# One graph-attention kernel on one core: transposes grouped ahead of their copies, layer 1's value loads on ScalarE's queue, pools in another order, late tiles started two steps apart

## The chip, the cores and the metric

The kernel runs on one core of one Trainium2 chip. The metric is the device time of one launch in microseconds (us). A profile is one further execution taken by the hardware profiler; its times count from the start of its span. The engines are TensorE (PE, with its weight loads as PEld), VectorE (DVE), ScalarE (ACT), GpSimd (POOL) and SyncE (SP, which here only issues transfers). "SPq", "ACTq" and "POOLq" are the transfers that these engines issue.

## The reference

x is 2708 x 256, adj is 2708 x 2708 and sparse with a full diagonal. Two layers follow each other, each as `x = layernorm(x + layer(x, adj))`.

```python
# layer 0, two steps n of: top-p attention and a walk over the graph
q = Xa @ W1.T @ W2.T;  k = Xa @ W3.T
probs = softmax(q @ k.T)
A = probs cut to the smallest set of each row with mass 0.9, rows rescaled
R = adj + I, rows rescaled
Xf = R @ Xf;  Xa = A @ Xa
Z = Z + Xf @ U1[n].T + Xa @ U2[n].T
# after both steps: layernorm(x + Z) * g + b
# layer 1, four heads of 64: graph attention
Wh = einsum('nd,hdo->nho', x, W)
e = leaky_relu(s_i[:, None] + s_j[None, :])       # s_i, s_j: Wh times a
attention = softmax(where(adj != 0, e, -inf))
h_prime = einsum('ijh,jho->iho', attention, Wh)
```

## The kernel before

**Tiles.** The 2708 rows are cut into 22 tiles: 16 of 128 rows and 6 of 110. For transposes they are taken in groups of up to four tiles of the same height (`groups`, six of them). All matrix work is in float32; one matmul of the program shows as two records on PE.

**Layer 0, start.** `query_weights` (L606 on) folds W1 and W2. Then `turn_x` transposes x, group by group: for each of the two halves c of the 256 columns, up to four PE transposes write half c of a two-bank PSUM tile `lg`, and a copy brings that half to SBUF (c = 0 by ScalarE, c = 1 by VectorE, both L1091). `project` (L619 on) multiplies the turned group by the weights (L631) and copies keys out by VectorE (L635) and queries by ScalarE (L636). The loop turns group n + 1 before it projects group n, so that the PE has transposes while the copies of group n run. `lg` and the projections' PSUM tile `tr` have two buffers each.

**Layer 0, the two steps.** In each step, for each tile, PE turns the scores (L240) and multiplies (L258, `att`), with the walk's matmuls (L901) dealt out between; ScalarE, VectorE and GpSimd find the cut of the coming tiles. This runs from about 74 us to 1229 us.

**Late tiles.** Tiles 18 to 21 (`LATE = 4`) are not finished inside layer 0. Each is a generator, `prepared(t)` (L1330 on), and each call of `beside` (L1344 on) moves it one step. Six steps are two layer norms, done by ScalarE and GpSimd alone (`layernorm_beside`, L141 on, and `norms`, L181 on); the seventh transposes the tile's x on PE (L160) and copies it (L162); the eighth multiplies it by layer 1's weights (L166), after which ScalarE writes `sb`, `tj`, `s_src` and the four heads' values (L170 to L176) and stores the values to DRAM (L179). `verdict` (L1127 on) is a fifth generator, a check of layer 0's shortcuts, nearly all on VectorE. Before the change late tile k lets k calls pass and then starts, and `verdict` lets 4 pass.

**Layer 1.** Destinations are taken in three groups g of 8, 8 and 6 tiles; for each g all 22 source tiles j are gone through, two at a time ("a pair" below). `mask` (L1286 on) loads tile j's values `v[j]` from DRAM (only for g = 0, L1290) and then calls `neighbours`, which loads the block of adj (L1220) into one of three buffers `blk` and makes it 0 or 1 by two passes of ScalarE (Sign L1221, Square L1222). `weights` makes four tiles `pt` per source tile on VectorE (L1302), in a ring of three. `values` multiplies them by v (L1313), `denominators` by `sb` (L1323). A pair is: `beside`, `weights(n+2)`, `mask(n+3)`, values and denominators of both tiles, `beside`, `weights(n+3)`, `mask(n+4)`. So `beside` is called twice a pair, once at each side of the pair's matmuls.

**Who sets the order.** The lines run under a manual schedule for PE, ACT, DVE and POOL: within one such block each of these engines keeps the order of the program text. SP is not among them; where its transfers stand is the framework's choice, and so is how the two blocks (layer 0 and layer 1) are merged at their seam. In the program before, the first three blocks of adj are loaded and turned into masks while layer 0's last tile is still attended to.

**Pools.** SBUF pools lie one behind the other in the order in which they are opened. Layer 1's pools are opened after those of layer 0 are closed and lie over the same addresses; the first use of a new pool waits for the last uses of all old pools that it overlaps. Before: `pj` (the `pt` tiles) lies over part of w0, over keep (xm, qT, kT1) and over the front of tpp (the turned scores `eT`); `keep1` (the values v) lies over keepb (`ba`, the values of step 1's attention) and wk.

Of the kernel before, what the change touches and what calls it, by code (L numbers as in the profile page):

```python
# [37 lines left out]
HELD, WAITING = 6, 4  # L38
# [6 lines left out]
def kernel(  # L45
# [16 lines left out]
    nc = tc.nc  # L62
# [5 lines left out]
    NT = (N + P - 1) // P  # L68
# [48 lines left out]
    LATE = 4  # L117
# [37 lines left out]
    def sources(t, pool, room, queue=nc.sync):  # L155

        m = rows[t]
        tp = room()
        for c in range(DC):
            nc.tensor.transpose(tp[:, c, :m], xe[:m, t, c * P : (c + 1) * P], ident[:m, :m])  # L160
        xT = pool.tile([P, DC, P], F32, name="xT")
        nc.scalar.copy(xT[:, :, :m], tp[:, 0:DC, :m])  # L162
        yield
        wp = room().rearrange("p a b -> p (a b)")
        for c in range(DC):
            nc.tensor.matmul(  # L166
                wp[:m, : D + 2 * H], xT[:, c, :m], wx[:, c, :],
                start=(c == 0), stop=(c == DC - 1),
            )
        nc.scalar.activation(sb[:m, t, :], wp[:m, D : D + H], AF.Exp)  # L170
        nc.scalar.activation(tj[:m, t, :], wp[:m, D : D + H], AF.Exp, scale=NEG_SLOPE - 1.0)
        nc.scalar.copy(s_src[:m, t, :], wp[:m, D + H : D + 2 * H])
        vt = pool.tile([P, D], F32, name="cs")
        for h in range(H):
            cols = slice(h * FO, (h + 1) * FO)
            nc.scalar.activation(  # L176
                vt[:m, cols], wp[:m, cols], AF.Copy, scale=sb[:m, t, h : h + 1]
            )
        queue.dma_start(vd[t][:m], vt[:m])  # L179

    def norms(t, xt, norm=layernorm, other=None):  # L181

        m = rows[t]
        hh = xe[:m, t, 0:D]
        h2 = hh if other is None else other()[:m]
        yield from norm(h2, hh, m)
        nc.gpsimd.tensor_mul(h2, h2, g_sb[:m])  # L187
        nc.gpsimd.tensor_add(h2, h2, xt[:m])  # L188
        yield
        yield from norm(hh, h2, m)  # L190
        yield
        if t < NT - LATE:
            yield
# [331 lines left out]
    def fast_layer0(ep, adjp):  # L525

        l0 = ExitStack()

        heldp, finp, rowp, w0, keep, tpp, sortp, keepb, wk = (
            l0.enter_context(tc.tile_pool(name=name, bufs=bufs))  # L530
            for name, bufs in (
                ("heldp", HELD), ("finp", 2), ("rowp", 2), ("w0", 1), ("keep", 1),
                ("tpp", 3), ("sortp", 1), ("keepb", 1), ("wk", 1),
            )
        )
        ps_lg, ps_wk, ps_at, ps_tr = (
# [543 lines left out]
        def turn_x(grp):  # L1080
            k = rows[grp[0]]
            w, c0 = k * len(grp), off[grp[0]]
            tp = ps_lg.tile([P, 2, CHUNK], F32, name="lg")
            for c in range(DC):
                for q, t in enumerate(grp):
                    nc.tensor.transpose(
                        tp[:, c, q * k : (q + 1) * k], xm[:k, t, c * P : (c + 1) * P],
                        ident[:k, :k],
                    )
                copy = nc.vector.tensor_copy if c else nc.scalar.copy  # L1090
                copy(x_turned[:, c, c0 : c0 + w], tp[:, c, :w])  # L1091
            return c0, w

        with tc.manual_schedule(engines=engines):
            query_weights()
            ahead = turn_x(groups[0])
            for n in range(len(groups)):
                c0, w = ahead
                if n + 1 < len(groups):
                    ahead = turn_x(groups[n + 1])  # L1100
                pj = ps_tr.tile([P, 4, P], F32, name="tr").rearrange("p a b -> p (a b)")
                project(
                    0, c0, w, pj, x_turned[:, :, c0 : c0 + w],
                    nc.scalar.copy, nc.vector.tensor_copy,
                )
# [87 lines left out]
    def layer1(ep, adjp, r=None, verdict=None):  # L1193
        l1 = ExitStack()

        pp, pj, rp, keep = (
            l1.enter_context(tc.tile_pool(name=name, bufs=bufs))
            for name, bufs in (("pp", 2), ("pj", 1), ("rp", 1), ("keep1", 1))
        )
        DEEP = 3  # L1200
        ps_u = l1.enter_context(tc.tile_pool(name="ps_u", bufs=2, space=PSUM))
# [12 lines left out]
        def neighbours(g, j):  # L1214

            k = rows[j]
            i0, i1 = off[spans[g][0]], off[spans[g][-1] + 1]
            bar = adjp.tile([P, NT - HT, P], F32, name="blk")
            bar = bar.rearrange("p t d -> p (t d)")[:k, : i1 - i0]
            nc.sync.dma_start(bar, adjT[off[j] : off[j + 1], i0:i1])  # L1220
            nc.scalar.activation(bar, bar, AF.Sign)  # L1221
            nc.scalar.activation(bar, bar, AF.Square)  # L1222
            if j in spans[g]:
                own = bar[:, off[j] - i0 : off[j + 1] - i0]
                nc.vector.tensor_tensor(own, own, ident[:k, :k], op=ALU.max)
            return bar
# [59 lines left out]
        def mask(n):  # L1286
            if n < len(order):
                g, _, j = order[n]
                if g == 0:
                    nc.sync.dma_start(  # L1290
                        v[j][: rows[j]].rearrange("p h o -> p (h o)"), vd[j][: rows[j]]
                    )
                masks[n] = neighbours(g, j)
# [36 lines left out]
        def prepared(t):  # L1330

            yield from norms(
                t, x_late[:, t - NT + LATE, :], layernorm_beside,
                lambda: pp.tile([P, D], F32, name="h2", bufs=4),
            )
            yield from sources(t, pp, aux, nc.scalar)


        late = []
        if verdict:  # L1340
            late += [[k, prepared(NT - LATE + k)] for k in range(LATE)]
            late.append([LATE, verdict(aux)])
        rest, running = [], []
        def beside(g, i):  # L1344

# [19 lines left out]
        for n in range(DEEP):  # L1365
            mask(n)
# [3 lines left out]
        for n in range(0, len(order), 2):  # L1370
            g, i, j = order[n]
            beside(g, i)
            weights(n + 2)
            mask(n + 3)
            if i == 0:
                acc = [
# [7 lines left out]
            for u in (n, n + 1):  # L1384
                for k in range(2):
                    values(u, (2 * k, 2 * k + 1))
                    if last and u > n:
                        for c, (c0, w) in enumerate(cuts[g]):
                            copy = nc.scalar.copy if c == 0 else nc.vector.tensor_copy
# [3 lines left out]
            if last:  # L1393
                for c, (c0, w) in enumerate(cuts[g]):
                    copy = nc.scalar.copy if c == 0 else nc.vector.tensor_copy
# [3 lines left out]
            else:  # L1399
                beside(g, i + 1)  # L1400
            weights(n + 3)
            mask(n + 4)
        assert not late

# [10 lines left out]
    with ExitStack() as both:  # L1415

        adjp = both.enter_context(tc.tile_pool(name="adjp", bufs=3))
        ep = both.enter_context(tc.tile_pool(name="ep", bufs=3))
        left = fast_layer0(ep, adjp)
        with tc.manual_schedule(engines=engines):  # L1420
            layer1(ep, adjp, *left)
    flag = nc.values_load(bad[0:1, 0:1])
    with tc.If(flag > 0):
        general_layer0()
        with ExitStack() as again:
            adjp = again.enter_context(tc.tile_pool(name="adjp", bufs=3))
            ep = again.enter_context(tc.tile_pool(name="ep", bufs=3))
            layer1(ep, adjp)
# [45 lines left out]
```

## Time and profile before

Three runs took 1595.8, 1595.95 and 1597.88 us; the median is 1595.95 us. The profiled execution took 1593.14 us, its span is 1591.3 us.

| engine | busy us | share of the span | instructions |
|---|---|---|---|
| PE | 1542.3 | 97% | 8029 |
| DVE | 1202.5 | 76% | 3651 |
| ACT | 798.9 | 50% | 1462 |
| POOL | 429.1 | 27% | 884 |

How to read it: PE is busy nearly all the time, so time is lost or won where it is not: at the start (before 34 us), at the seam between the layers (about 1229 to 1345 us) and at the very end. The rows of groups by line have the busy time, the mean of one, and the idle time before them with what ended it. In the timeline, equal instructions that follow each other are one row: start, length, engine, line, operation, tiles, how many records, and in brackets the idle time before the row and what ended it. A granted clock below 1.00 in a stretch means that PE ran slower for a part of it.

### The profile page before, as it was taken

The numbers are of one execution on the slowest core, as the hardware profiler recorded it, in microseconds if no ns is written. First come the engines' busy times: TensorE is split into PE (matmuls) and PEld (weight loads), VectorE is DVE, ScalarE is ACT, GpSimd is POOL, SyncE is SP. The second block draws the span as 40 slices with busy tenths as digits, with TensorE's granted clock in tenths as the row PEclk, the third lists the DMA queues.
The fourth block names the chain that finished last, engine by engine and source line by source line (L and its number), as shares of the span: only waits on it lengthen the run. The fifth ranks groups of instructions, "written<-read, shape, count | busy, mean of one in ns | idle before, by whom it ended". The sixth has DMA issues, their size and how long they took to land. (4 is left out here: it accounts for less than half of the span.)

```text
span 1591.3 us, 23822 instructions
## 1 busy us (share of the span) xinstructions
PE 1542.3 (97%) x8029; PEld 1037.7 (65%) x8029; DVE 1202.5 (76%) x3651; ACT 798.9 (50%) x1462; POOL 429.1 (27%) x884
## 2 busy tenths in 40 slices
PE   6999999999998999999999999999999999999994
PEld 3477777777776888787787788887787333333342
DVE  2777677767408876878779888888884978999995
ACT  2444444444335455555555556556643454456473
POOL 1311000000022222232224454534441720033133
PEclk9999999999999999999999999999999999999997
DMA  5200000000134333333333334433344434334331
GB/s 139 78 13 14 12 9 12 10 9 10 42 94 124 86 100 82 98 76 78 80 102 94 100 107 107 111 104 93 78 101 130 130 102 139 93 105 133 85 100 43
DMA packets 172494, 128.27 MB, mean 81 GB/s; under 512 B 44342, under 2 KB 161804, under 8 KB 172362
## 3 DMA queue, kind: packets, MB, share of 16 engines
q1 hardware_dynamic: 165030, 114.63, 26.9%
q0 software_dynamic: 3648, 9.26, 1.8%
q10 hardware_dynamic: 3684, 2.76, 0.5%
q8 instruction: 65, 1.06, 0.3%
q14 instruction: 67, 0.55, 0.1%
HBM read 111.78 MB, written 13.46 MB: 79 GB/s over the span
## 5 line engine op out<-in xcount | busy, mean ns | idle before, releaser
L245 ACT COPY eT<-tr 128x512 f32<-128x512 f32 (+5 forms) x264 | 141.2, 535 | 275.8 <-PE tr L240 273.1
L686 ACT ACTIVATE junk<-e,minus,rth 128x2708 bf16<-128x2708 f32 (+1 forms) x88 | 232.8, 2646 | 36.1 <-POOL rth L718 35.2
L258 PE MATMUL att<-xm,eT 128*128 128x256 f32 (+3 forms) x968 | 230.9, 380 | 0.4 <-ACT xa L1030 0.4
L258 PE MATMUL att<-ba,eT 128*128 128x256 f32 (+3 forms) x968 | 230.8, 379 | 0.3 <-ACT eT L245 0.2
L901 PE MATMUL walk<-xe,blk 128*128 128x257 f32 (+3 forms) x968 | 225.3, 384 | 5.0 <-DVE xf L915 5.0
L901 PE MATMUL walk<-xm,blk 128*128 128x256 f32 (+3 forms) x968 | 222.0, 380 | 1.0 <-DVE xw L974 1.0
L1313 PE MATMUL acc<-pt,v 128*64 128x512 f32 (+3 forms) x1056 | 216.3, 555 | 2.4 <-DMA v<-v 2.2
L901 PEld LDWEIGHTS walk<-xe,blk 128*128 128x128 f32 (+3 forms) x968 | 178.5, 187 | 50.3 <-issue 12.6
L1302 DVE SCALAR_TENSOR_TENSOR pt<-e,tj,blk 128x1024 f32<-128x1024 f32 (+3 forms) x176 | 187.1, 1128 | 20.3 <-PE att L258 8.7
L901 PEld LDWEIGHTS walk<-xm,blk 128*128 128x128 f32 (+3 forms) x968 | 177.7, 186 | 34.5 <-issue 4.9
L258 PEld LDWEIGHTS att<-xm,eT 128*128 128x128 f32 (+3 forms) x968 | 169.6, 186 | 22.1 <-ACT xa L1030 0.8
L258 PEld LDWEIGHTS att<-ba,eT 128*128 128x128 f32 (+3 forms) x968 | 169.5, 186 | 22.0 <-ACT eT L245 0.8
L665 ACT ACTIVATE e<-lg 128x1024 f32<-128x1024 f32 (+1 forms) x132 | 121.0, 921 | 110.6 <-PE lg L661 107.0
L1313 PEld LDWEIGHTS acc<-pt,v 128*64 128x64 f32 (+1 forms) x1056 | 75.6, 139 | 133.2 <-issue 107.5
L766 DVE MAX8 cand<-e 128x8 f32<-128x170 f32 (+1 forms) x352 | 89.6, 323 | 90.5 <-ACT e L665 90.4
L240 PEld LDWEIGHTS tr<-ident,e 128*128 128x128 f32 (+3 forms) x968 | 115.1, 138 | 56.3 <-issue 21.0
L240 PE MATMUL tr<-ident,e 128*128 128x128 f32 (+3 forms) x968 | 147.1, 271 | 0.7 <-ACT xe L952 0.3
L1302 DVE SCALAR_TENSOR_TENSOR pt<-r,tj,blk 128x1024 f32<-128x1024 f32 (+1 forms) x88 | 110.0, 1313 | 5.8 <-PE acc L1323 3.0
L1323 PE MATMUL acc<-pt,sb 128*32 128x512 f32 (+3 forms) x1056 | 106.8, 545 | 0.0
L766 DVE MAX8 cand<-scr 128x8 f32<-128x97 f32 (+1 forms) x616 | 102.3, 245 | 0.0
L1221 ACT ACTIVATE blk<-blk 128x1024 f32<-128x1024 f32 (+3 forms) x66 | 63.1, 956 | 70.2 <-DMA blk<-in_adjT_dram 57.1
L915 DVE TENSOR_TENSOR xf<-walk,xe 128x257 f32<-128x257 f32 (+1 forms) x22 | 9.4, 426 | 110.8 <-PE walk L901 110.8
(237 smaller groups left out, 1976.2 us busy)
## 6 DMA issues: line engine op xcount, KB each, us to landing
blk<-in_adjT_dram SPq DMA_DIRECT2D x32, 704.0 KB
blk<-in_adjT_dram SPq DMA_DIRECT2D x32, 512.0 KB
blk<-in_adjT_dram SPq DMA_DIRECT2D x48, 330.0 KB
blk<-in_adjT_dram SPq DMA_DIRECT2D x32, 320.0 KB
blk<-in_adjT_dram SPq DMA_DIRECT2D x12, 605.0 KB
blk<-in_adjT_dram SPq DMA_DIRECT2D x12, 440.0 KB
blk<-in_adjT_dram SPq DMA_DIRECT2D x18, 283.6 KB
c<-cs POOLq DMA_DIRECT2D x32, 128.0 KB, 2.0
```

Of the source, the lines that this page charges most:

```text
L240: nc.tensor.transpose(tr[: rows[t], q, :m], e[:m, off[t] : off[t + 1]], ident[:m, :m])
L245: copy(eT[:k, : len(grp), :m], tr[:k, : len(grp), :m])
L258: nc.tensor.matmul(acc, eT[: rows[t], q, :m], value(t), start=(t == 0), stop=(t == NT - 1),)
L665: nc.scalar.activation(halves[:m, :, c0 : c0 + w], lg[:m, :, :w], AF.Exp, accum_out=zp[:m, n : n + 1],)
L686: nc.scalar.activation(junk[:m], e[:m], func, scale=rth, bias=minus1[:m], accum_out=acc)
L766: nc.vector.max(cand[:, n, :], src[:m, n * size : min(N, (n + 1) * size)])
L901: nc.tensor.matmul(ac[:m, :w], blk[: rows[j], j - j0, :m], cur[: rows[j], j, 0:w], start=(j == 0), stop=(j == NT - 1),)
L915: nc.vector.tensor_add(xf[:m], ac[:m, : D + 1], xe[:m, t, :])
L1221: nc.scalar.activation(bar, bar, AF.Sign)
L1302: nc.vector.scalar_tensor_tensor(pt[:k, :gw], targets[g][h // 2][:k, h % 2, :gw], tj[:k, j, h : h + 1], bar, op0=ALU.max, op1=ALU.mult,)
L1313: nc.tensor.matmul(acc[h // 2][c][q * FO : (q + 1) * FO, :w], v[j][:k, h, :], probs[n][h][:k, c0 : c0 + w], **at,)
L1323: nc.tensor.matmul(acc[2][c][h * 32 : (h + 1) * 32, :w], sb[:k, j, h : h + 1].to_broadcast([k, 32]), probs[n][h][:k, c0 : c0 + w], **at,)
```

## The change

Four edits. In layer 0 the pool `tpp` is opened before `w0` and `keep` rather than after them, and in layer 1 `rp` is opened before `pj`. In `turn_x` all transposes of a group, both halves, come before its two copies. In `mask` the load of `v[j]` is issued by ScalarE rather than by SP. Late tile k lets 2k calls of `beside` pass rather than k, and `verdict` 8 rather than 4. No arithmetic changes, and each engine has the same number of compute instructions as before; 22 issues of transfers move from SP to ScalarE.

```diff
@@ fast_layer0
-        heldp, finp, rowp, w0, keep, tpp, sortp, keepb, wk = (
+        heldp, finp, rowp, tpp, w0, keep, sortp, keepb, wk = (
             l0.enter_context(tc.tile_pool(name=name, bufs=bufs))
             for name, bufs in (
-                ("heldp", HELD), ("finp", 2), ("rowp", 2), ("w0", 1), ("keep", 1),
-                ("tpp", 3), ("sortp", 1), ("keepb", 1), ("wk", 1),
+                ("heldp", HELD), ("finp", 2), ("rowp", 2), ("tpp", 3), ("w0", 1),
+                ("keep", 1), ("sortp", 1), ("keepb", 1), ("wk", 1),
             )
         )
@@ turn_x
                         tp[:, c, q * k : (q + 1) * k], xm[:k, t, c * P : (c + 1) * P],
                         ident[:k, :k],
                     )
-                copy = nc.vector.tensor_copy if c else nc.scalar.copy
+            for c, copy in enumerate((nc.scalar.copy, nc.vector.tensor_copy)):
                 copy(x_turned[:, c, c0 : c0 + w], tp[:, c, :w])
             return c0, w
@@ layer1
-        pp, pj, rp, keep = (
+        pp, rp, pj, keep = (
             l1.enter_context(tc.tile_pool(name=name, bufs=bufs))
-            for name, bufs in (("pp", 2), ("pj", 1), ("rp", 1), ("keep1", 1))
+            for name, bufs in (("pp", 2), ("rp", 1), ("pj", 1), ("keep1", 1))
         )
@@ mask
                 if g == 0:
-                    nc.sync.dma_start(
+                    nc.scalar.dma_start(
                         v[j][: rows[j]].rearrange("p h o -> p (h o)"), vd[j][: rows[j]]
                     )
@@ layer1
         if verdict:
-            late += [[k, prepared(NT - LATE + k)] for k in range(LATE)]
-            late.append([LATE, verdict(aux)])
+            late += [[2 * k, prepared(NT - LATE + k)] for k in range(LATE)]
+            late.append([2 * LATE, verdict(aux)])
```

## The prediction

> **What bounds the kernel now.** I read the page first, then busy time by stretch, then the timelines of PE, DVE and ACT at the start and at the seam of the layers.
>
> ```profile
> PE 1542.3 (97%) x8029; PEld 1037.7 (65%) x8029; DVE 1202.5 (76%) x3651; ACT 798.9 (50%) x1462; POOL 429.1 (27%) x884
> ```
> ```profile
> 10.00:20.00 10.00, 8.14 (x25) 4.50 (x24) 2.76 (x4) 1.75 (x3) 0.80 (x1) 1.00 0.98 246
> 20.00:34.00 14.00, 9.05 (x42) 5.50 (x40) 4.46 (x8) 3.13 (x7) 2.07 (x4) 1.00 0.13 28
> 34.00:74.00 40.00, 40.00 (x107) 16.59 (x108) 27.88 (x100) 19.00 (x52) 12.54 (x27) 1.00 0.23 76
> ```
>
> PE (the second number) is full from 34 us on, and the same table has 325.1 of 326 us from 74 to 400. So what the start saves is carried to the end. At the start PE waits for copies:
>
> ```profile
> 9.04 1.97 PE L1086 MATMUL lg<-ident,xm 128*128 128x128 f32 x8 [0.68 <-ACT ba L1091]
> ...
> 18.70 1.88 PE L631 MATMUL tr<-ba,wkqk 128*128 128x512 f32 x4
> ...
> 22.58 0.66 PE L1086 MATMUL lg<-ident,xm 128*128 128x128 f32 x4 [1.56 <-ACT ba L1091]
> ```
>
> The second half's transposes wait for the first half's copy, since both are one tile. Six such waits in all: 0.68, 0.68, 1.18, 1.56, 0.89, 1.45, together 6.44 us. (The first projection, at 12.59, took 3.62 us; the third waits 1.05 for a copy of qT in its middle.) Layer 0's last matmul ends at 1229.3. The seam on PE, the first pt on DVE, and the clock (the number after PE's busy time and count) in two stretches of 1 us:
>
> ```profile
> 1231.49 10.48 PE L1313 MATMUL acc<-pt,v 128*64 128x512 f32 x32 [2.19 <-DMA v<-v]
> ...
> 1267.86 0.41 PE L160 MATMUL aux<-ident,xe 110*128 110x110 f32 x2 [1.15 <-ACT xe L153]
> ...
> 1282.18 1.14 PE L166 MATMUL aux<-wx,xT 128*110 128x264 f32 x4 [2.05 <-ACT xT L162]
> ...
> 1283.61 8.56 PE L1313 MATMUL acc<-pt,v 110*64 110x512 f32 x32
> ```
> ```profile
> 1229.40 31.65 DVE L1302 SCALAR_TENSOR_TENSOR pt<-e,tj,blk 128x1024 f32<-128x1024 f32 x24 [8.67 <-PE att L258]
> ```
> ```profile
> 1284.00:1285.00 1.00, 1.00 (x4) 0.50 0.29 115
> ...
> 1287.00:1288.00 1.00, 1.00 (x8) 1.00 0.38 111
> ```
>
> An undisturbed pair takes 7.09 us of values and 3.57 of denominators. The first pair is set by DVE (8 tiles pt). The pairs at 1283.61 and 1299.93 take 1.47 and 1.69 more: their clock was 0.50 for 3.4 us, after a wait of 2.05 or, at 1298.74 for the next xT, of 1.74. The pair at 1333.60 takes 1.16 more (a late mask). Losses at the seam after the first pair: 1.15 + 2.05 + 1.74 + 1.47 + 1.69 + 1.16 = 9.3 us.
>
> **What the skill says.** "TensorE: Matmul & The Clock Gate", Part 1: the clock is halved by default, is freed after about 3.4 us of sustained work, and is halved again after an idle window of that length, windows running freely. The trace agrees: projections take 0.9 us a matmul record until 16.8 us and 0.47 after, and each halved stretch lasts 3.4 us. But a window half idle was enough (1.74 of 3.4), while 1.56 at 21 us and 1.15 at 1266.7 were not. "DMA: Bandwidth & Descriptors", Issuing engines are not separate DMA queues: another issuing engine saves only issue time; SP's loads of v take 0.43 to 0.47 each. "SBUF — State Buffer", two separate sides: a VectorE operation with two SBUF inputs and a GpSimd one lock each other out. Here three of the first tiles pt take 1.75 instead of 1.27, beside GpSimd's L981 and L982.
>
> **Transposes first.** The order of the changed program has eight transposes, then the ACT copy, and the DVE copy that waits for ACT's. I rebuild the chain with the measured pieces. Turning a group: 1.97 cold, 1.3 warm (0.66 a half); projecting: 3.62 cold, 1.88 warm; copies 0.58 (ACT) and 0.69 (DVE), one after the other, 1.4 with their handovers. Group 0 is turned 7.25 to 9.2, group 1 to 11.2, its projection runs to 14.8 (its copies ended at 10.6), group 2 to 16.1, projection 1 to 18.0, group 3 to 19.3, projection 2 to 22.8 with the wait for qT (1.35 here), group 4 to 23.9, projection 3 to 25.8, group 5 to 26.5, the last two projections (2.4) to 28.9. Before they ended at 34.1: 5.2 us saved. The loads of x don't stop this: transfers that SP issued at 10.0 and 10.6 us had waited for groups 2 and 3. Group 1 may be 0.3 late (landed by 9.5). The clock may come sooner, as PE works without a gap from 7.25: half of a projection warm is 0.8 more. I take 5.8; bounds 4.5 (cold to 16.8) and 7.
>
> **Other space.** Nothing comes earlier: in the built order the first pt still waits for the last att matmul, because `pj` now reaches over `ba`, which that matmul reads. Zero. rp's transfers wait only for that matmul too, 80 us earlier.
>
> **v on ScalarE.** The load of tile 8 waits for the same matmul (it lies over old space), and ScalarE keeps its program order: Sign and Square of the first three blocks, which ran at 1206.9, 1217.7 and 1223.7, hidden, now stand behind it. After 1229.3: xa to 1229.8, the issue 0.3 to 0.57, Sign and Square 2.1, so pt starts at about 1232.6 instead of 1229.40: 3.2 late. GpSimd's L981 and L982 are over by then, which could give three times 0.48 back; 8 tiles pt then take 8 x 1.216 = 9.75 instead of the 10.55 to 1239.95: 0.8. The first pair is DVE's, so +2.4 (2 to 3.3). PE's longer idle halves its clock, covered while it waits for DVE: each pt gives it 0.88 of work at full clock in 1.22. The other loads stand ahead of each mask: two a pair, 0.7 of ScalarE's 10.6; masks have more room (worked out next). SP's blocks are no longer behind loads of v: the late mask at 1333.6 goes, -1.2.
>
> **Late tiles two apart.** A tile is transposed at its seventh call and multiplied at its eighth, so tile 0's transposes (T0) stand before the fourth pair, M0 after it, T1 before the fifth, and so on, with no xT wait: -2.05 -1.74. T0 is ready some 4 us before its turn: -1.15. But the same call that makes M_k also ends the norm of tile k+1, and on ScalarE that norm's last operation (L153) stands behind M_k's outputs, which wait for PE. T_k+1 waits for L153, and the next pair stands behind T_k+1. From ACT's timeline:
>
> ```profile
> 1296.85 0.17 ACT L170 ACTIVATE sb<-aux 110x4 f32<-110x4 f32 x1 [7.42 <-PE aux L166]
> ...
> 1297.06 0.93 ACT L176 ACTIVATE cs<-aux,sb 110x64 f32<-110x64 f32 x4
> 1298.01 0.29 ACTq L179 DMA_DIRECT2D v<-cs  x1
> 1298.34 0.34 ACT L162 COPY xT<-aux 128x220 f32<-128x220 f32 x1 [0.36 <-ACT cs L176]
> ```
>
> M started at 1295.67: L170 comes 1.18 after, ScalarE is free 1.49 later, L153 takes 0.60, 0.05 to PE: T_k+1 starts 3.32 after M_k, where without the wait it would start 0.98 after (1278.79 to 1279.77). So 2.34 us three times (T1, T2, T3), +7.0. Idle of 2.2 to 2.3 lies wholly in one 3.4 window one time in three, and covers half of one in somewhat over half of all cases: 1.7 halved windows of 1.6 us, +2.7 (0 to 5). Before lost 3.2 that way in the profile; waits of 2.05 and 1.74 should do so about half the time, 1.4 to 1.6.
>
> Masks after M_k: ScalarE is free 3.3 after it, then two norm steps, a load, Sign and Square (4 together), so DVE starts tile n+4 some 8 us after M_k and ends 5.5 later, while PE needs it 14 to 15 after M_k, plus the 2.3: 2 to 4 us of room. Verdict's small operations on DVE (0.2 each) lie in it.
>
> **Sum.** -5.8 (start) +2.4 (first pt) -1.15 -3.8 -1.2 +7.0 = -2.55; halved windows +2.7 -3.2 against the profiled execution: -3.0, so 1590.1 against its 1593.14 (span 1591.3 and 1.8 around it). The median of the three runs is 2.8 above that; three runs differ by 2.1, as much as a window or so. With 1.5 for the windows of an average run before, it is -1.3. I take -2: **1594.0**.
>
> **Rivals.** *A: the waits ahead of T1 to T3 are short or hardly touch the clock, and the start warms early.* -7 and windows of 0 to 1 us give -6 to -8: about 1588.5. For it: 1.56 of idle cost no window. Against: L153's place in ScalarE's order is fixed. *B, slower: masks become late.* ScalarE takes 22 issues, sits 7 us at each M_k, and loads of v stand between it and each mask. If issues cost over 1 us (SP's 0.43 speak against it) or norm steps wait for GpSimd, the room of 2 to 4 us after M_k goes and DVE starves PE; at 3 us beyond the room in each of three pairs it is +9, 1601; it decides from about 5 us in all. *C: the start's gain isn't there* because projections wait for the two copies in a row: they have the next group's transposes (1.3) and a projection as cover against 1.4; then the 5.8 go: about 1599.8. *D: other space does nothing*, part of the main case.
>
> **How the numbers follow.** 0.2% is 3.2 us, about what can be told from no change. Main case, -4.5 to +1, 0.55; A 0.28; B 0.09; C and the rest 0.08. The main case's lower end is past -3.2 in a fifth of its cases and A's nearly all: faster 0.35, same 0.55, slower 0.10. The range takes in A and half of C: 1588 to 1598.5; the main case alone is 1591.5 to 1597.
>
> **What would show it.** Right: the first scores (L661) begin near 28.5 instead of 34.10; pt starts some 3.2 after the last att instead of at once; three rows L160 with a wait of 2.2 to 2.4 for ACT xe L153, no wait for xT; some clock of 0.50 after them. Wrong: no L153 waits (A), idle of DVE for ACT blk L1222 with PE waiting for pt beside it (B), waits at L631 for ba (C).

## The result, and the profile after

The changed kernel takes 1586.55 us, median of four runs (1586.19 to 1587.31); the kernel before took 1595.88 beside it (four runs, 1595.21 to 1597.88). The ratio is 0.994, interval 0.9923 to 0.9957: 9.3 us faster. The forecast was 1594.0 with a range of 1588 to 1598.5, so the result lies 1.5 below the range. The sign was right with a chance of 0.35; the likeliest case, no difference, was wrong.

The profiled execution of the changed kernel took 1586.25, span 1584.4. Against the profiled execution before (span 1591.3) that is 6.9 less, not 9.3; the other 2.4 come back below. The page's first line, then busy time by stretch (stretch, its length, busy time of PE, PEld, DVE, ACT, POOL with counts, granted clock, share and rate of the transfers):

```profile
PE 1537.4 (97%) x8029; PEld 1036.2 (65%) x8029; DVE 1201.2 (76%) x3651; ACT 799.5 (50%) x1462; POOL 440.9 (28%) x884
```
```profile
10.00:20.00 10.00, 8.43 (x34) 5.05 (x32) 4.49 (x7) 3.35 (x6) 1.33 (x2) 1.00 1.04 252
20.00:34.00 14.00, 13.98 (x52) 7.05 (x53) 5.40 (x15) 6.67 (x16) 4.31 (x10) 1.00 0.22 55
```

PE has the same 8029 records but 4.9 us less busy time, so part of the gain is not a wait removed but work done at a faster clock. And PE is full from 20 us on, not from 34. The timeline of PE shows the start and the seam (start, length, instruction, and in brackets the wait ahead of it):

```profile
7.40 3.67 PE L1086 MATMUL lg<-ident,xm 128*128 128x128 f32 x16
10.87 2.98 PE L631 MATMUL tr<-ba,wkqk 128*128 128x512 f32 x4
13.68 1.04 PE L1086 MATMUL lg<-ident,xm 128*128 128x128 f32 x8
14.56 1.88 PE L631 MATMUL tr<-ba,wkqk 128*128 128x512 f32 x4
...
26.02 1.99 PE L661 MATMUL lg<-junk,qT 64*128 64x512 f32 x8
...
1225.22 10.30 PE L1313 MATMUL acc<-pt,v 128*64 128x512 f32 x32 [4.11 <-DVE pt L1302]
...
1249.61 9.21 PE L1313 MATMUL acc<-pt,v 128*64 128x512 f32 x32
...
1276.58 0.41 PE L160 MATMUL aux<-ident,xe 110*128 110x110 f32 x2 [2.19 <-ACT xe L153]
...
1290.86 0.41 PE L160 MATMUL aux<-ident,xe 110*128 110x110 f32 x2 [2.21 <-ACT xe L153]
...
1305.14 0.41 PE L160 MATMUL aux<-ident,xe 110*128 110x110 f32 x2 [2.10 <-ACT xe L153]
```

The first scores begin at 26.02 instead of 34.10, 2.5 earlier than forecast: the first projection takes 2.98 instead of 3.62, and group 2 (13.68) keeps PE for 0.88 until the next row, where the forecast had 1.3. The three waits for L153 are there as forecast. No clock of 0.50 follows them here. But the third pair takes 9.21 for its values instead of 7.09, and nothing in the forecast says why. The timelines of DVE, of POOL and of ACT around it do:

```profile
1223.88 24.01 DVE L1302 SCALAR_TENSOR_TENSOR pt<-e,tj,blk 128x1024 f32<-128x1024 f32 x20 [11.34 <-ACT blk L1222]
1251.96 15.39 DVE L1302 SCALAR_TENSOR_TENSOR pt<-e,tj,blk 128x1024 f32<-128x1024 f32 x12 [4.07 <-ACT blk L1222]
```
```profile
1234.98 12.96 POOL L149 TENSOR_SCALAR lb_sq<-lb_sq 110x1 f32<-110x1 f32 x1 [6.13 <-ACT h L148]
```
```profile
1248.89 0.60 ACT L153 ACTIVATE h<-xe,lb_nb,lb_rs 110x256 f32<-110x256 f32 x1 [9.39 <-POOL lb_nb L151]
...
1249.80 1.04 ACT L1221 ACTIVATE blk<-blk 128x1024 f32<-128x1024 f32 x1
```

GpSimd's L149 handles 110 single numbers. It took 0.85 before and takes 12.96 here, and it ends at 1247.94, 0.05 after DVE's row of 20 tiles pt ends. ScalarE's L153 waits 9.39 for what follows it, the Sign of the sixth block (1249.80) stands behind L153, and DVE waits 4.07 for that mask. Spans on POOL are rough in a profile; the wait of ScalarE confirms this one.

Both spans taken apart:

| part | before | after | difference |
|---|---|---|---|
| end of layer 0's last matmul | 1229.30 | 1221.10 | -8.20 |
| from there to the start of the 11th pair | 126.64 | 127.92 | +1.28 |
| the rest of the span | 235.36 | 235.38 | 0 |

So in these two profiles the seam, where I had forecast most of the uncertainty, costs 1.3 more, and the whole gain is the start's.

### The profile page after: what moved, and what is told of

The parts are those of the page before. It is cut to its first block, busy times and chain, and to the rows that moved or that the text cites. A ratio compares the mean times of both kernels' runs of the same rounds, so it can differ in the third digit from the quotient of the medians.

```text
span 1584.4 us, 23826 instructions
## 1 busy us (share of the span) xinstructions
PE 1537.4 (97%) x8029; PEld 1036.2 (65%) x8029; DVE 1201.2 (76%) x3651; ACT 799.5 (50%) x1462; POOL 440.9 (28%) x884
## 5 line engine op out<-in xcount | busy, mean ns | idle before, releaser
L784 DVE MAX8 top<-work 128x8 f32<-128x128 f32 (+3 forms) x242 | 82.4, 340 | 8.3
```

The lines of the kernel that those rows point to most:

```text
L784: nc.vector.max(top[:, k : k + 8], work if k else flat)
```

## The experiments

Beside them the kernel before was run again: median 1593.05 of 31 runs in the first series, 1595.78 of 28 in the second and 1596.16 of 23 in the third, each on another chip. Its runs reach from 1589.39 to 1601.28; those of the changed kernel in two series from 1586.19 to 1588.01. One profile of the kernel before is therefore a weak base, and I read ratios for times and profiles for places.

The numbers of all profiles, from PE's timeline: start of the first scores; end of the last `att`; from it to the first pair; third pair (its start to the fourth's); pairs 4 to 8; ninth pair; the seam to the 11th pair's start; and GpSimd's first L149 (with masks first, L146).

| kernel | scores | att end | to pair 1 | pair 3 | pairs 4-8 | pair 9 | seam | GpSimd |
|---|---|---|---|---|---|---|---|---|
| before | 34.10 | 1229.30 | 2.19 | 12.14 | 65.40 | 11.75 | 126.64 | 0.85 |
| changed | 26.02 | 1221.10 | 4.12 | 13.05 | 65.19 | 10.59 | 127.92 | 12.96 |
| changed, again | 26.08 | 1221.14 | 4.11 | 13.05 | 66.89 | 10.59 | 129.62 | 12.87 |
| transposes first alone | 24.68 | 1220.14 | 2.25 | 15.82 | 63.69 | 11.99 | 128.85 | 12.12 |
| gaps filled | 32.71 | 1229.04 | 2.15 | 15.82 | 62.06 | 13.73 | 128.97 | 12.71 |
| late two apart alone | 34.23 | 1229.22 | 2.19 | 13.05 | 68.53 | 10.58 | 129.51 | 11.91 |
| v on ScalarE alone | 34.13 | 1229.22 | 4.16 | 15.76 | 62.23 | 13.78 | 130.91 | 12.78 |
| changed, v on SP | 26.00 | 1221.08 | 2.28 | 13.04 | 68.84 | 10.59 | 129.83 | 12.75 |
| changed, reversed | 26.08 | 1221.16 | 4.11 | 16.10 | 60.94 | 10.59 | 126.71 | 12.86 |
| changed, masks first | 25.71 | 1220.86 | 4.11 | 14.80 | 68.58 | 10.59 | 133.41 | 13.01 |
| before, no GpSimd | 35.88 | 1232.38 | 2.04 | 10.93 | 63.57 | 12.38 | 124.23 | - |
| changed, no GpSimd | 24.73 | 1219.87 | 4.12 | 10.92 | 68.54 | 10.58 | 129.14 | - |
| deferred outputs | 24.86 | 1220.05 | 4.11 | 13.06 | 59.53 | 10.59 | 122.27 | 12.87 |
| deferred, first v on SP | 25.94 | 1221.38 | 2.15 | 10.93 | 58.60 | 10.59 | 117.46 | 0.69 |

**Transposes first alone.** Only this edit on the kernel before:

```diff
-                copy = nc.vector.tensor_copy if c else nc.scalar.copy
+            for c, copy in enumerate((nc.scalar.copy, nc.vector.tensor_copy)):
                 copy(x_turned[:, c, c0 : c0 + w], tp[:, c, :w])
```

> The kernel before with only the transposes of a group put ahead of its copies. Theory (from the profile after, where the first scores begin at 26.02 us instead of 34.10): the start alone is worth 8.1 us and PE carries it to the end, so 8 us faster than before (ratio 0.995), L661 first at about 26.0, the seam of the layers as before with its three late waits (1.15, 2.05, 1.74). Rival 1, the size in my prediction: 5.8 us (ratio 0.9964), L661 at about 28.5. Rival 2: part of the start's gain in the changed kernel came from another edit; then L661 begins later than 26.5.

Measured: 1586.08 us, ratio 0.9952 (0.9936 to 0.9968). Of PE's timeline:

```profile
10.62 1.88 PE L631 MATMUL tr<-ba,wkqk 128*128 128x512 f32 x4
...
24.68 1.99 PE L661 MATMUL lg<-junk,qT 64*128 64x512 f32 x8
```

Here even the first projection runs at full clock, and the first scores come 9.4 earlier than before. In the nine profiles with transposes first it takes 1.88 (three of them) or 2.66 to 2.98 (six), in the four of the old order without a filler 3.62. The theory's 8.1 was low for the start of this execution; at the seam, where GpSimd's long L149 appears, 2.2 are lost again. The interval of the times still holds rival 1's 0.9964; it is the profile that speaks against it (24.68, not 28.5).

**Gaps filled.** The kernel before, with work for PE in its first two gaps:

```diff
                 copy(x_turned[:, c, c0 : c0 + w], tp[:, c, :w])
+                if c == 0 and grp[0] < 8:
+                    idle = ps_at.tile([P, CHUNK], F32, name="att")
+                    for _ in range(7):
+                        nc.tensor.transpose(idle[:, :P], ident, ident)
```

> The kernel before with seven transposes of the unit matrix into an unused PSUM tile in each of the first two gaps of PE at the start (0.68 us each, between the first half's transposes and the second's, groups 0 and 1). Theory: it was the two gaps that kept the clock halved until 16.8 us; filled, PE is at full clock by 13.4 at the latest, the first projection takes 1.9 to 3.0 us instead of 3.62, and the first scores begin 0.8 to 2.5 earlier than 34.1 although no wait for a copy is removed. Rival: the clock comes at a fixed time after the start of work whatever the gaps; then the first projection still takes 3.6 and the scores begin at 34 or later.

```profile
8.25 1.70 PE L1095 MATMUL att<-ident 128*128 128x128 f32 x7
9.74 1.92 PE L1086 MATMUL lg<-ident,xm 128*128 128x128 f32 x8
11.45 1.22 PE L1095 MATMUL att<-ident 128*128 128x128 f32 x7
...
12.94 1.88 PE L631 MATMUL tr<-ba,wkqk 128*128 128x512 f32 x4
...
32.71 1.99 PE L661 MATMUL lg<-junk,qT 64*128 64x512 f32 x8
```

The first filler costs more than its gap (second half at 9.74 instead of 9.04), and still the first projection takes 1.88 instead of 3.62 and the scores come 1.39 earlier, with the copies' later waits untouched. So, in this one execution, filling the gaps of 0.68 freed the clock: they had kept it halved. Little of the 1.39 reaches the end of layer 0: the last `att` ends at 1229.04 instead of 1229.30, and at 1220.07 PE has waited 0.91 for `eT`. (The one time, 1595.12, says nothing: its seam has the long L149.)

**Late two apart alone.** The last two lines of the change, on the kernel before.

> The kernel before with only the late tiles two calls apart. Theory: T0's wait of 1.15 and the two xT waits (3.8) go, three waits of 2.2 for xe L153 come (+6.5), and halved windows that before has (1.5 on average) mostly go: between -1 and +1.5 us against before, no difference that can be told. Rival, as in my prediction: these waits halve the clock in one to two windows, +2.7 more: +3 to +4. Second rival: the waits are not made by this edit alone but only together with v on ScalarE; then no L153 waits and -5.

Measured: 1594.65, ratio 1.001 (0.9998 to 1.0021), about no difference; an interval of -0.3 to +3.3 us holds part of the theory's range and part of the first rival's. The second rival fell: the three waits come from this edit alone (PE's timeline). From the first of them on the clock is 0.50 for 6.8 us, so that pair's values take 9.94 instead of 7.09:

```profile
1283.24 0.63 PE L160 MATMUL aux<-ident,xe 110*128 110x110 f32 x2 [2.47 <-ACT xe L153]
1283.80 9.94 PE L1313 MATMUL acc<-pt,v 110*64 110x512 f32 x32
...
1300.59 0.41 PE L160 MATMUL aux<-ident,xe 110*128 110x110 f32 x2 [2.21 <-ACT xe L153]
...
1314.85 0.41 PE L160 MATMUL aux<-ident,xe 110*128 110x110 f32 x2 [2.09 <-ACT xe L153]
```

**v on ScalarE alone,** with the old pools (`nc.sync.dma_start` to `nc.scalar.dma_start` in `mask`).

> The kernel before with only the load of v moved to ScalarE's queue (old pools). Theory: Sign and Square of the first three blocks stand behind the load of tile 8's v, which waits for the last att matmul; the first pt comes 2.6 us after that matmul's end instead of at once, the first pair ends 1.7 later, and the late mask of the ninth pair (1.2) goes: +0.5 us, at most +2. Rival: the load on ScalarE's queue costs nothing in front (pt at once) because the old pools let it go earlier: -1.2. Second rival: GpSimd is locked out by the first pt tiles for 10 us or more as in the profile after, and a mask is late by 2: +2.5 to +4.

Measured: 1599.47, ratio 1.0038 (1.0026 to 1.005): slower, and by more than the second rival's upper end. The pt tiles start 2.77 after the last `att` (1231.99 less 1229.22), with old pools as with new; L149 takes 12.78 and the third pair 15.76. And the late mask of the ninth pair, which the forecast put down to loads of v in SP's queue, is there with these loads gone:

```profile
1331.44 1.06 ACT L1221 ACTIVATE blk<-blk 128x1024 f32<-128x1024 f32 x1 [12.10 <-DMA blk<-in_adjT_dram]
```

The pair takes 13.78. In SP's queue that block stands behind the transfers of `shared` and of r (L215 and L223, issued from 1314.99 to 1322.68). With late tiles two apart, and v still on SP, the stall is gone (10.58 in the table). So the right edit for the 1.2 is the late tiles', not v's. The profile has 4.3 us more seam than the one before; the medians differ by 6.4. The other 2 lie between this profile and its own runs: it took 1597.49, 2.0 below their median, while the profile of before lies at the median of its runs in this series (1593.14 and 1593.05).

**The changed kernel again, and with v back on SP.**

> The changed kernel itself once more, beside the kernel before on this chip. Theory: about 1586.5, its runs within 1 to 1.5 us of each other, GpSimd's L149 takes some 13 us in the profile and ends with DVE's row of 20 tiles pt. Rival: the difference of 9.3 us was partly a slow draw of the kernel before; then the ratio is about 0.9955 to 0.996 here (7 us), as the two profiled executions (1593.14 and 1586.25) say.

> The changed kernel with the loads of v back on SP's queue (transposes first, other pools and late tiles two apart kept). Theory: pt starts right at the last att's end instead of 2.7 later, the first pair begins 1.75 sooner, and a late mask of 1.2 in the ninth pair may return: 0.5 to 2 us faster than the changed kernel. Rival: the loads on ScalarE's queue are what the gain over my forecast came from (SP's queue no longer holds blocks of adj back in the first pairs); then this kernel is 2 to 6 us slower than the changed one.

Measured: 1587.52, ratio 0.9947 (0.9932 to 0.9963), and with v on SP 1587.59, ratio 0.9942 (0.9929 to 0.9956). So the change brings some 8 us here as well, though the interval also holds the 7 us of the rival. Moving v makes no difference that these runs can tell: with v on SP the first pair comes 1.83 sooner, but in its profile T1 waits 2.47 and halved clocks follow T1 and T3. Neither the theory (0.5 to 2 faster) nor the rival (2 to 6 slower) came. For the changed kernel itself, one stretch of 1 us in the second profile, and the same in the first:

```profile
1307.00:1308.00 1.00, 1.00 (x6) 0.39 (x4) 0.64 (x3) 1.00 (x3) 0.00 (x0) 0.50 0.59 168
```
```profile
1307.00:1308.00 1.00, 1.00 (x6) 0.29 (x4) 0.68 (x3) 1.00 (x3) 0.00 (x0) 1.00 0.75 217
```

The same kernel, the same wait of T3 (2.11 and 2.10), and once the clock is halved after it, which costs 1.69 (the seventh pair takes 13.47 instead of 11.78), once not.

**Reversed order, and masks first.** Two edits of the changed kernel: the late tiles advanced in reverse within a call (`for part in list(late)[::-1]`), and each `mask` call put ahead of the `beside` that stood before it.

> The changed kernel with one more edit: the late tiles are advanced in reverse order within a call, so that the last norm operation of tile k+1 (L153) stands ahead of M_k's outputs on ScalarE. Theory: the three waits of PE at L160 (2.19, 2.21, 2.10 us, together 6.5) are made by that order alone; they go, and the kernel is 6.5 us faster than the changed one, 1580. Rival: the waits move, T waits for GpSimd's part of the norm or a mask comes late behind it, and 2 us or less are gained: 1584.5 or more.

> The changed kernel with each mask's load, Sign and Square put ahead of the call of beside that stood before it, so that they no longer stand behind a norm operation (L153) that waits for GpSimd. Theory: GpSimd is kept out by DVE's pt tiles for 12 to 13 us, L153 waits 9 for it and the sixth tile's mask waits behind L153; with the mask ahead the third pair takes 7.09 for its values instead of 9.21, and 2 us are gained; the three waits at L160 stay. Rival: without the late mask DVE keeps GpSimd out for longer, the norm of tile 18 comes later and T0 waits for it: no gain or a loss.

Reversed: 1584.63, ratio 0.9943 (0.9926 to 0.9961), not to be told from the changed kernel's 0.994 and 0.9947. T1 and T2 wait no more and T3 waits 1.11 for L176, but tile 18's norm now comes last in each call, T0 waits 3.31 and a halved clock follows: the rival, in its first half. Masks first: 1595.23, ratio 0.9994 (0.998 to 1.0008), some 8 slower than the changed kernel. The rival's loss came, but only in part by its route (POOL, then DVE):

```profile
1234.73 13.01 POOL L146 TENSOR_SCALAR lb_nm<-lb_sq 110x1 f32<-110x1 f32 x1 [11.81 <-ACT h L145]
```
```profile
1250.43 21.12 DVE L1302 SCALAR_TENSOR_TENSOR pt<-e,tj,blk 128x1024 f32<-128x1024 f32 x16 [2.80 <-ACT blk L1222]
```

GpSimd is kept out no longer than before; the kept-out operation is an earlier one of the same norm. The mask of the sixth tile is still late, now behind L148, and DVE waits 2.80 for it instead of 4.07. T0 waits 2.36 as the rival said, and halved clocks follow. The seam is 5.5 longer than the changed kernel's; another 3.6 are lost in the very last two pairs (9.18 and 8.28 instead of 6.95 and 6.94), of which neither theory nor rival speaks.

**GpSimd taken out of the late norms.** `nm`, `rs` and `nb` by ScalarE and L187, L188 left out, as the expectations say. These two kernels compute other values and serve only to show what GpSimd's part costs; they also have less work in each norm. A part of the edit, the branch that the late tiles take:

```diff
+        if own:
+            nc.scalar.activation(nm, sq, AF.Copy, scale=-1.0 / D)
+            yield
+            nc.scalar.activation(dst, src, AF.Square, bias=nm, accum_out=sq)
+            nc.scalar.activation(rs, sq, AF.Exp, scale=-0.5 / D)
+            nc.scalar.activation(nb, nm, AF.Copy, scale=rs)
```

> The kernel before with GpSimd taken out of the late tiles' norms: the mean, the power and the product of L146 to L151 are replaced by three operations of ScalarE (an exponential in place of the power, so other values), and the product with g and the sum with x (L187, L188) are left out. Theory: most runs of the kernel before lose 3.7 to 5.5 us at the seam because GpSimd's L149 is kept out for 12 to 13 us while DVE makes the first 20 tiles pt, and L153 and the masks stand behind it; without it the third pair takes 10.6 instead of 15.8, T0's wait of 1.2 goes too, and the runs fall by 3 to 6 us and lie closer together (the two xT waits stay). Rival: the long L149 is an artefact of the record, the masks are late for another reason (their transfers): no difference.

> The changed kernel with GpSimd taken out of the late tiles' norms in the same way (an exponential in place of the power, the product with g and the sum with x left out). Theory: the third pair's late mask goes (13.05 to 10.6 from the third pair to the fourth), the three waits at L160 stay as they are: 2.5 us faster than the changed kernel. Rival as for the kernel before: no difference.

On the kernel before: 1590.55, ratio 0.9974 (0.9963 to 0.9984), about 4 us faster and its 19 runs within 5.4 instead of 10.4 us, as expected; the third pair, 15.8 in the old spacing with the long L149, takes 10.93. DVE's row and, at the start, a piece of bad luck of this execution:

```profile
1232.47 29.96 DVE L1312 SCALAR_TENSOR_TENSOR pt<-e,tj,blk 128x1024 f32<-128x1024 f32 x24 [8.67 <-PE att L268]
```
```profile
28.37 3.29 PE L641 MATMUL tr<-ba,wkqk 128*128 128x512 f32 x4
```

DVE has no break at the sixth tile. The projection at 28.37 takes 3.29 instead of 1.90: in the old order the clock can be lost a second time during the start, which may be another part of the old kernel's scatter. On the changed kernel: 1586.41, ratio 0.9945 (0.9923 to 0.9967). The late mask went as expected (10.92 instead of 13.05), but two of the three waits brought a halved clock in this profile, and next to nothing remained of the 2.5 expected.

**Deferred outputs,** on the changed kernel, in `sources`:

```diff
+        if queue is not nc.sync:
+            yield
         nc.scalar.activation(sb[:m, t, :], wp[:m, D : D + H], AF.Exp)
```

> The changed kernel with the outputs of a late tile's multiplication (L170 to L179) put one call later than its matmuls, so that on ScalarE they stand behind the last norm operation (L153) of the next tile and not ahead of it, while the order of the tiles within a call stays. Theory: the three waits at L160 (2.19, 2.21, 2.11) go and nothing takes their place; with them goes any halved clock window after them: 6.5 to 8 us faster than the changed kernel, ratio to before about 0.990. Rival: as in the reversed order, the norms come later for GpSimd's sake and T0 or a mask is late: 2 us or less.

> As the kernel with deferred outputs, and the loads of v of the first three tiles issued by SP again, so that the first three masks need not wait for layer 0's last matmul. Theory: pt starts at the last att's end, the first pair begins 1.9 sooner, and this is kept to the end now that the late tiles' waits are gone: another 1.5 to 2 us, ratio to before about 0.989. Rival: the third pair's late mask, which GpSimd's 13 us set, takes it all back: no difference.

Measured: 1579.61, ratio 0.9905 (0.9884 to 0.9927). The second adds `(nc.sync if n < DEEP else nc.scalar).dma_start` for v: 1577.18, ratio 0.9892 (0.9867 to 0.9916). Both beat both kernels. PE's timeline of the first, then DVE's and POOL's of the second:

```profile
1273.17 0.35 PE L160 MATMUL aux<-ident,xe 110*128 110x110 f32 x2
...
1285.73 0.41 PE L160 MATMUL aux<-ident,xe 110*128 110x110 f32 x2 [0.54 <-ACT xe L153]
```
```profile
1221.48 51.73 DVE L1304 SCALAR_TENSOR_TENSOR pt<-e,tj,blk 128x1024 f32<-128x1024 f32 x40 [8.93 <-PE att L260]
```
```profile
1233.82 0.69 POOL L149 TENSOR_SCALAR lb_sq<-lb_sq 110x1 f32<-110x1 f32 x1 [7.63 <-ACT h L148]
```

Of 2.19, 2.21 and 2.10 there remain 0, 0.54 and 0.36 (the last for a copy of `line`). That the waits were ScalarE's order is shown, and the seam is 5.65 shorter than the changed kernel's. In the second kernel's profile L149 was let in and DVE made 40 tiles without a break. So of the 4.8 by which its seam is shorter still, 1.96 are the first pair's, which the edit aimed at, and 2.13 the third pair's, which is luck of this execution; the rival of the late mask was not put to the test. Its four runs scatter from 1574.73 to 1578.93, those of the first from 1579.47 to 1579.68.

## Why the prediction was wrong

By its own steps, profiled execution against profiled execution:

| step | forecast | measured | how |
|---|---|---|---|
| start | -5.8 | -8.20 | end of the last `att` |
| first pt later | +2.4 | +1.75 | 4.12 - 2.19, and the first pair 13.80 instead of 13.98 |
| T0 no longer waits | -1.15 | -1.15 | no wait at 1262.32 |
| xT waits gone | -3.8 | -3.79 | 2.05 + 1.74 |
| ninth pair's mask | -1.2 | -1.16 | 10.59 instead of 11.75 |
| T1 to T3 wait for L153 | +7.0 | +6.50 | 2.19 + 2.21 + 2.10 |
| halved clocks of before gone | -3.2 | -3.16 | 1.47 + 1.69 |
| halved clocks after | +2.7 | 0 | every pair at 7.09 but the first (DVE's) and the third |
| late mask, third pair | none | +2.12 | 9.21 - 7.09 |

They sum to -3.05 and to -7.09; the spans differ by 6.9.

**The start was mis-sized, above all in the price of a turned group.** The order of the rebuilt chain held; its pieces were too long. From row start to row start in the changed kernel, groups 2 to 5 take 0.88, 0.88, 0.76 and 0.38, together 2.90, where the forecast had 1.3, 1.3, 1.1 and 0.7, together 4.4. That is 1.5 of the 2.9 by which the chain (28.9) missed 26.02. The forecast took the length of a row, 0.66, for half a group. But a row can end after the next one has started, as the profile of before already had it:

```profile
22.58 0.66 PE L1086 MATMUL lg<-ident,xm 128*128 128x128 f32 x4 [1.56 <-ACT ba L1091]
23.08 1.28 PE L631 MATMUL tr<-ba,wkqk 128*128 128x330 f32 x4
```

The row would end at 23.24; the next starts at 23.08, 0.50 after it. The cold groups 0 and 1 were too long as well (3.47 instead of 3.95). The clock's share is 0.8, at the first projection (2.81 from start to start instead of 3.6); the forecast named 0.8 and took 0.6. That this share was no more is luck of the execution: in three of the nine profiles the first projection is at full clock at once. The end of the last `att` came 7.9 to 9.4 earlier in the nine profiles than in before, all beyond the bound of 7. Rival A ("the start warms early"), with its 1588.5, was the nearest in number, but only in part for its reasons: the waits ahead of T1 to T3 were not short.

**Halved clocks: the size was a mean, and the case is a lottery.** 0 in the first profile, 1.7 in the second of the same kernel. The forecast of 0 to 5 holds; taking 2.7 in full was too high for these two, while late tiles two apart alone lost more than 2.7 with the same three waits.

**The late mask was not forecast.** Rival B's result (DVE idle for ACT blk L1222 while PE waits for pt) came in small, 2.1, but at the third pair and not after M_k, and by another cause: the forecast saw GpSimd and DVE lock each other out in three pt tiles of 0.48 and counted that as 0.8 gained. It did not ask what happens to the next small GpSimd operation when DVE's row has no break. "SBUF — State Buffer" of the Trainium skill, two separate sides, which the forecast cites, has one such operation wait for the whole of the other. A wait of that kind agrees with the traces; but one pt takes 1.2 us, and that GpSimd was kept out for some ten of them in a row stands only here.

**"SP's blocks are no longer behind loads of v: -1.2" was right in amount and wrong in cause.** With v moved alone the ninth pair takes 13.78; with late tiles two apart alone it takes 10.58.

**The base.** The forecast took -3.0 against the profiled execution for about -2 against the median and explained the 2.8 between them by "a window or so". The change of the profiles is -6.9, of the medians -9.3: 2.4 lie there. Ten of the twelve profiles in which GpSimd does these norms have an operation of 11.9 to 13.0 us; the profile of before that I worked from is one of the two that don't. With it, the old spacing costs 15.8 in the third pair, the new one 13.05. So the late tiles' edit gains more in an execution with the long L149 than in the one I had. That the early execution was an unusual one is an inference from these profiles, not a measurement of its runs, and the first series speaks against it: there the median of 31 runs of before, 1593.05, is what the profiled execution took.

The sum of the miss, 7.4: 2.4 (start), 0.65 (first pt), 0.5 (L153), 2.7 (clocks), less 2.1 (late mask), 1.0 (from -3.0 to -2), 2.4 (base), less about 0.2 that no step holds. So the steps that failed are three terms of the sum that were mis-sized (the start, -5.8 for -8.20; the halved clocks after the waits, +2.7 for 0 to 1.7; the base, 2.4) and one put at nothing, the late mask (+2.1), which worked the other way.

**The other rivals.** Rival C fell (no wait at L631 for ba). Rival D stands: with old pools and v on ScalarE pt starts 2.77 after `att`, with new ones 2.78; with new pools and v on SP the first pair comes 2.28 after it, with old ones 2.19. No run has the other space alone; at these places it does nothing.

**The edits do not add up.** Alone they give ratios of 0.9952, 1.001 and 1.0038, together not 1.000 but 0.9947. Much of that is one loss counted three times. Each of the three profiles has the long L149, and the profile of before has not: with old spacing and v on SP its seam is 126.64, and with the long L149 (gaps filled) 128.97, 2.3 more. The three spans differ from before by -6.8, +2.7 and +4.4, together +0.3; against a before with those 2.3 they would come to about -6.7 (an estimate), where the two profiles of the changed kernel have -9.2 and -7.4 on the same base. So a third pair of 15.8 belongs to the long L149 in the old spacing, wherever v is loaded, and a ninth of 12 to 13.8 to the old spacing; v's own price is the first pair's 1.9. Whether the runs of before behind the medians had the long L149 isn't known. What stays open is why L149 is kept out in one execution and let in in another; no run here varied that by itself.

## What to carry to other kernels

When a chain is rebuilt from a profile, price its pieces from row start to row start, not by the rows' lengths: 0.88 against 1.3 for one turned group here. While the clock is still halved at a kernel's start, a gap of PE of 0.68 us can cost more than itself: price it with the next projections at both clocks. Where an engine keeps program order, put what waits for PE behind what PE will wait for; moving a tile's outputs one call later took the ratio from 0.9947 to 0.9905 here (each against the kernel before on its own chip). And when a profile lies 2.8 us from the median of its runs, find out what differs before working with its waits to 0.1.

## What the runs showed of the hardware that I had not expected

A GpSimd operation on 110 x 1 numbers took 11.91 to 13.01 us in ten profiles, each time ending within 0.11 us of the end of DVE's row of 20 pt tiles, and 0.69 and 0.85 in the two others, beside DVE rows just as unbroken. Of the wait of T3, 1.84 us lay in one window of the clock (the edges taken from the halved stretches, 3.413 apart) in the first profile of the changed kernel and 1.89 in the second; only the second was followed by 0.50. In the kernel before 1.74 had been enough, in a window that held four short matmuls besides, so idle time as the records show it is not all that counts.
